# Flamingo block with sparse experts: the last three expert tiles behind a branch, and each tile's rows added to the output by two DMAs of half rows

## The chip, the cores and the metric

The kernel runs on one core of one Trainium2 chip. The metric is the device time of one execution in microseconds (us). Engines are named as in the profile: PE does matmuls (PEld loads its weights), DVE, ACT and POOL are the vector, scalar and GpSimd engines, and SP only issues DMAs here. Each engine takes its instructions in the order in which they stand in its queue; engines and DMAs wait for each other through semaphores.

## The reference

Two gated blocks run over x of 4 x 512 tokens by 512 numbers, each a mixing step and a feed-forward step, all added to x. The first three steps (a gated int8 product, a ternary feed-forward and an attention of 16 heads) don't change here. The last step is the one the change touches: a mixture of experts, in which each of the 2048 tokens takes its two best of eight experts.

```python
logits = router_in @ router_w.T
probs = jax.nn.softmax(logits, axis=-1)
topw, topi = jax.lax.top_k(probs, TOP_K)                    # TOP_K = 2, E = 8
topw = topw / jnp.sum(topw, axis=-1, keepdims=True)
cw = jnp.zeros((T, E), flat.dtype).at[jnp.arange(T)[:, None], topi].add(topw)
g = jnp.einsum('td,edf->tef', flat, gate_w)                 # D = 512, F_E = 256
u = jnp.einsum('td,edf->tef', flat, up_w)
a = jax.nn.silu(g) * u
expert_out = jnp.einsum('tef,efd->ted', a, down_w)
y = jnp.einsum('ted,te->td', expert_out, cw) * SCALE
...
x = x + jnp.tanh(g_ffn[1]) * y
```

## The kernel before, in words

The first 1340 us or so are the first three steps and the attention, with PE full nearly throughout. What follows concerns the experts' stage, which begins while the attention's last heads still run and lasts to the end.

**Tiles.** The 4096 pairs of a token and an expert are sorted by expert into tiles of P = 128 rows. How many rows an expert has is known only at run time, so there are NSEG = 39 tiles, the most that could be needed; every tile's work is written out in the program, and the tile's expert number is read into a register (L1086) to pick the weights. Tiles 0 to 15 (part "a") are full tiles of rows from the first twelve token tiles, so that they can start before the last batch is through the attention. Tiles 16 to 38 (part "b") take the rest. `sort` runs once for each part, in steps (`yield`) beside other work, and leaves in `found[j]` the row numbers `ids` (128 on partitions, one column for each tile), the expert `owner_i` and a mask `owned` of the experts. Rows of a tile that belong to nobody get a number out of bounds.

**One tile's way.** `fetch`/`gather` (L1072, an indirect DMA that POOL issues) brings 128 rows of 512 numbers and 8 weights from the table `xtab` into `xg`, of which there are eight buffers. `weigh_rows` (L1081, L1082, on DVE) picks each row's weight of its expert. The rows are turned, either by PE (`by_tensor`, L1184 and a copy on ACT) or by DVE transposes and 16 SP DMAs (L576, L1175) for four tiles together. `hide` does the eight gate/up matmuls (L1089), the silu on ACT (L1090) and the product with the row's weight on DVE (L1091). `turn_hidden` turns the hidden rows on PE (L1184, copy on DVE L1185). `expert_out` does the four down matmuls (L1211), copies the sum to `y` on ACT (L1215; three buffers), and POOL issues an indirect DMA that adds the 128 rows of 512 numbers, 2 KB each, into `out` (L1216). Row numbers out of bounds are skipped.

**Order.** The loop at L1245 writes the order out by hand: in step j it fetches tiles ahead of their use (4 or 10 tiles), does the gate/up matmuls of tile j, turns the rows of tile j + 1 if PE does that, turns the hidden rows of tile j - 1 and puts out tile j - 2. In the last steps the order is bent so that the last tile's gate/up matmuls stand behind tile 36's and 37's down matmuls. On POOL's queue an add is followed by the gathers of that step.

**Adds in a chain.** Two tiles can hold the same token, so an add must not run while another is under way. The list `written` holds the last add, and the next one waits until that has landed (`add_manual_dep`). The first add of each part also waits for the stores of x to `out` that it adds to.

**The framework.** Semaphores are set by a tile framework, which also tracks reads and writes of tensors itself and puts waits between instructions that touch the same data.

Of the kernel before, what the change touches and what calls it, by code (L numbers as in the profile page):

```python
# [9 lines left out]
F32 = mybir.dt.float32  # L10
BF16 = mybir.dt.bfloat16
AF = mybir.ActivationFunctionType
ALU = mybir.AluOpType
AX = mybir.AxisListType

P = 128
B, S, D = 4, 512, 512
NT = S // P
# [23 lines left out]
NE, TOPK, FE = 8, 2, 256  # L42
# [3 lines left out]
TOK = B * S  # L46
TT = TOK // P
NSEG = (TOK * TOPK + NE * (P - 1)) // P
NA, TA = 16, 12
NB = NSEG - NA  # L50
ROW = D + NE
F32R = mybir.dt.float32r
I32 = mybir.dt.int32
# [3 lines left out]
def kernel(  # L57
# [21 lines left out]
    nc = tc.nc  # L79

    cp = ctx.enter_context(tc.tile_pool(name="const", bufs=1))
# [17 lines left out]
    def place_in(w, at, n):  # L99

        flat = w.rearrange("p e k f -> p (e k f)")
        return flat[:, at : at + n]
# [37 lines left out]
    def acc_tile():  # L140
        sums_in[0] += 1
        return bank(4 + sums_in[0] % 4)

    def small(n, tag):
        return sm.tile([P, n], F32, tag=tag, name=tag)
# [63 lines left out]
    with tc.tile_pool(name="q8", bufs=1) as q8, tc.tile_pool(name="l0", bufs=2) as l0, tc.tile_pool(  # L209
        name="w0", bufs=1  # L210
# [420 lines left out]
    def load_queries(n):  # L631
        th = la.tile([P, ROW], F32, tag="wq", name="wq")
        th = th[:, : KD * HD].rearrange("p (k n) -> p k n", k=KD)
        nc.gpsimd.dma_start(th, wq[:, n * HD : (n + 1) * HD].rearrange("(k p) n -> p k n", p=P))  # L634
        return th
# [80 lines left out]

    xtab = dram.tile([TOK + P, ROW], F32, name="xtab")
    yacc = out.rearrange("b s d -> (b s) d")
    rwT = cp.tile([P, KD, NE], F32, name="rwT")
    before = cp.tile([P, NE, NE], F32, name="before")  # L720
    ones_b = cp.tile([P, P], BF16, name="ones_b")
# [10 lines left out]
    def router_constants():  # L732
# [24 lines left out]

        zero = place_in(gu, 4 * SLOT + 512, ROW)
        nc.gpsimd.memset(zero, 0.0)
# [5 lines left out]
    stores = []  # L765
# [93 lines left out]
    def exclusive(v, tag):  # L859

        lower = sm.tile([P, NE, NE], F32, tag="ahead", name="lower")
        nc.vector.tensor_tensor(lower, before, v.unsqueeze(1).to_broadcast([P, NE, NE]), ALU.mult)
        t = small(NE, tag)
        nc.vector.tensor_reduce(t, lower, AX.X, ALU.add)
        return t

    def tiles_of(nt, shift):

        ps = work_tile()
        nc.tensor.matmul(ps[:, :NE], lhsT=ones_b, rhs=past[:, nt, :], start=True, stop=True)  # L870
        t = small(NE, "tiles")
        nc.vector.tensor_scalar(t, ps[:, :NE], 1.0 / P, shift, ALU.mult, ALU.add)
        nc.vector.tensor_scalar(t, t, ROUND, None, ALU.add)
        nc.vector.tensor_scalar(t, t, -ROUND, None, ALU.add)
        return t
# [3 lines left out]
    def full_tiles():  # L879
# [10 lines left out]
        nc.vector.tensor_scalar(base, first, float(P), None, ALU.mult)  # L890
        return last, base, limit, (ALU.is_ge, FAR)

    def other_tiles():
        tiles = tiles_of(TT, (P - 1) / (2 * P))
        nc.vector.tensor_tensor(tiles, tiles, taken, ALU.subtract)
        first = exclusive(tiles, "first")
        nc.vector.tensor_scalar(first, first, float(NA), None, ALU.add)
        last = small(NE, "last")
        nc.vector.tensor_tensor(last, first, tiles, ALU.add)
        limit = small(NE, "limit")  # L900
        nc.vector.tensor_scalar(limit, taken, float(P), None, ALU.mult)
        base = small(NE, "base")
        nc.vector.scalar_tensor_tensor(base, first, float(P), limit, ALU.mult, ALU.subtract)
        return last, base, limit, (ALU.is_lt, -FAR)

    found = {}

    def sort(pool, part, nt, c0, n, spans):
# [30 lines left out]
        nc.vector.tensor_reduce(owner, done, AX.X, ALU.add)  # L939
        owner_i = cp.tile([P, n], I32, name=part + "owner_i")  # L940
        nc.vector.tensor_scalar(owner_i, owner, NE - 1.0, None, ALU.min)
        owned = cp.tile([P, n, NE], F32, name=part + "owned")
        nc.vector.tensor_tensor(
            owned,
            owner.unsqueeze(2).to_broadcast([P, n, NE]),
# [5 lines left out]
        for s in range(TOPK):  # L951
            mine = pool.tile([P, nt, NE], F32, tag=part + "mine", name="mine", bufs=1)
# [19 lines left out]
        for s in range(TOPK):  # L972
            mine = slice(s * nt, (s + 1) * nt)
# [31 lines left out]
        nc.vector.scalar_tensor_tensor(none, ps[:, :n], -1.0, none, ALU.add, ALU.add)  # L1005
        ids = cp.tile([P, n], I32, name=part + "ids")
        nc.vector.tensor_tensor(ids, none, ps[:, n : 2 * n], ALU.add)
        for j in range(n):
            found[c0 + j] = (ids[:, j : j + 1], owner_i[0:1, j : j + 1], owned[:, j, :])
        yield  # L1010


# [2 lines left out]
    def step_beside():  # L1015
        if beside:
            try:
                next(beside[0])
            except StopIteration:
                beside.pop(0)  # L1020
# [45 lines left out]

    def gather(j, xg):

        ids, _, owned = found[j]
        table = xtab[: TA * P, :] if j < NA else xtab[:, :]  # L1070
        tc.keep_in_program_order(
            nc.gpsimd.indirect_dma_start(xg, None, table, bass.IndirectOffsetOnAxis(ap=ids, axis=0))  # L1072
        )
        return xg, owned
# [21 lines left out]
    hidden, first = {}, {}  # L1096
# [17 lines left out]
    for i in range(LAST + 3):  # L1114
        b, n = divmod(i, NHEAD)
# [13 lines left out]
        if i == LAST:  # L1129
            while beside:  # L1130
                step_beside()
            for j in range(len(first_hid)):
                first_rows[j] = gather(j, la.tile([P, ROW], F32, tag="wq", name="xg"))
        if i > LAST:
# [13 lines left out]

    by_tensor = {j for j in range(NSEG) if j < 2 * NT or j // NT == NA // NT or j >= NSEG - NSEG % NT}
    blocks_of, turned_in, got = {}, {}, {}

    def fetch(j):
        got[j] = gather(j, mo.tile([P, ROW], F32, tag="xg", name="xg", bufs=8))

# [31 lines left out]
    def prepare(j):  # L1188
        if j in by_tensor and j not in hidden and j not in turned_in:
            dst = mo.tile([P, KD * P], F32, tag="xgT", name="xgT", bufs=2)  # L1190
            turned_in[j] = turn_by_tensor(got[j][0], KD, dst, nc.scalar.copy)
            weigh_rows(j, *got.pop(j))

    def hide(j):
        if j not in hidden:
            prepare(j)
            h = mo.tile([P, FE], F32, tag="hid", name="hid", bufs=3)
            hidden[j] = expert_in(j, turned_in.pop(j), h)

    def turn_hidden(j):  # L1200
        e, h = hidden.pop(j)
        hT = turn_by_tensor(h, NF, mo.tile([P, NF * P], F32, tag="hidT", name="hidT", bufs=3))
        waiting[j] = (e, hT)

    written = []

    def expert_out(j):
        e, hT = waiting.pop(j)
        ps = acc_tile()
        for f in range(NF):  # L1210
            nc.tensor.matmul(  # L1211
                ps, lhsT=hT[f], rhs=dn[:, bass.ds(e, 1), f, :], start=(f == 0), stop=(f == NF - 1)
            )
        y = mo.tile([P, D], F32, tag="y", name="y", bufs=3)
        nc.scalar.copy(y, ps)  # L1215
        add = nc.gpsimd.indirect_dma_start(  # L1216
            yacc,
            bass.IndirectOffsetOnAxis(ap=found[j][0], axis=0),
            y,
            None,  # L1220
            bounds_check=TOK - 1,
            oob_is_err=False,
            compute_op=ALU.add,
        )
        if j in (0, NA):
            written.extend(stores[-1:] if j else stores[: B - 1])
        for w in written:
            tc.add_manual_dep(
                add.ins,
                w.ins.name,  # L1230
                mybir.DependencyInfo(mybir.DependencyClass.Sync, mybir.DependencyReason.DATA),
                reason="adds to what is there",
            )
        written[:] = [add]

    beside += [route(B - 1, mo), sort(mo, "b", TT, NA, NB, other_tiles)]
    hidden.update(first)
    waiting = {}

    lead = {j: 4 if j in by_tensor else 10 for j in range(len(first), NSEG)}  # L1240
    TURN = 7
    to_fetch = sorted(lead, key=lambda j: (max(j - lead[j], 0), j))
    to_turn = [j for j in to_fetch if j not in by_tensor]

    for j in range(NSEG + 1):  # L1245
        known = NSEG if len(found) == NSEG else NA
        for t in [t for t in to_fetch if t - lead[t] <= j and t < known]:
            fetch(t)
            to_fetch.remove(t)
        while to_turn and to_turn[0] - TURN <= j and to_turn[0] in got:  # L1250
            turn_rows(to_turn.pop(0))


        if j < NSEG - 1:
            for i in range(NT) if j == 0 else (j,):
                hide(i)
        if j and j + 1 < NSEG:
            prepare(j + 1)
        if j:
            turn_hidden(j - 1)  # L1260
        for i in (j - 2,) if j < NSEG - 1 else (j - 2, j - 1) if j == NSEG - 1 else (j - 1,):
            if i >= 0:
                expert_out(i)
        if j == NSEG - 1:
            hide(j)
        step_beside()
        step_beside()
        if j == NA - 4:
            while beside:
                step_beside()  # L1270


# [33 lines left out]
```

## Time and profile before

| | |
|---|---|
| median of 3 runs | 1577.73 us (1575.53 to 1578.02) |
| the profiled execution | 1579.8 us, with a span of 1578.0 us |
| PE busy | 1493.4 us, 95% |
| DVE, ACT, POOL busy | 908.2, 559.0, 422.1 us |
| granted TensorE clock, mean | 0.989 |
| add of a tile, POOL's part (L1216) | 39 times, 1.55 to 1.63 us |
| first and last add start at | 1357.85 and 1570.03 us |
| gather of a tile, POOL's part (L1072) | 39 times, 0.94 to 1.05 us |
| copy of a tile's sum to y (L1215) | 0.586 us |

The span is the time from the profiled execution's first instruction to its last; the execution itself took 1.8 us more. "Busy" is the time in which an engine runs instructions; of an indirect DMA only the part in which POOL writes its descriptors counts as busy, and the flight of the data afterwards is seen only in who waits for it. In lists of waits, "A <- B: 115.6, 35, 11.0" says that A stood idle until B came, 115.6 us in total, 35 times, 11.0 us at the longest. In a timeline each line has its start, its duration, the instruction, and in brackets the idle time ahead of it and what ended that.

### The profile page before, as it was taken

To read this page: it belongs to the slowest core of one execution; us is meant where nothing else is said; L and a number is where in the kernel's file an instruction comes from. 1 tells how busy PE (TensorE), PEld (TensorE's weight loads), DVE (VectorE), ACT (ScalarE), POOL (GpSimd) and SP (SyncE) were. 2 spreads that over 40 slices of the span, in tenths; PEclk is the share of its full clock that TensorE was granted. 3 is DMA by queue.
4 is the path that set the end of the run, shared out by engine and by line. 5 is a ranking of instruction groups with operands and counts; after the bars stand their busy time and mean duration, and the time that the engine had idled before them with its cause. 6 is when DMAs were issued, how large, how long until landed. Compare 5 with 4: busy or idle time off the path is not lost. (4 is left out here: it accounts for less than half of the span.)

```text
span 1578.0 us, 16041 instructions
## 1 busy us (share of the span) xinstructions
PE 1493.4 (95%) x4339; PEld 750.1 (48%) x4348; DVE 908.2 (58%) x2350; ACT 559.0 (35%) x1150; POOL 422.1 (27%) x546
## 2 busy tenths in 40 slices
PE   4888898899999999999999999999999998999997
PEld 2444656666544444444444444444444443455563
DVE  5898737556175555575655675655777552643311
ACT  3554453434243333353333353333433331412111
POOL 2232314352311122141131141131231112345332
PEclk9999999999999999999999999999999999999999
DMA  8633111013355445485455575574675653656642
GB/s 296 217 118 129 47 40 61 28 41 101 126 161 140 140 137 161 134 221 151 123 158 138 148 203 140 132 188 132 191 199 134 162 129 88 166 112 141 127 75 34
DMA packets 111512, 211.90 MB, mean 134 GB/s; under 512 B 29296, under 2 KB 33392, under 8 KB 111424
## 3 DMA queue, kind: packets, MB, share of 16 engines
q0 software_dynamic: 33408, 98.54, 23.9%
q1 hardware_dynamic: 70224, 100.74, 22.9%
q10 hardware_dynamic: 7792, 11.60, 2.2%
q8 instruction: 37, 0.61, 0.2%
q14 instruction: 51, 0.42, 0.1%
HBM read 96.14 MB, written 35.72 MB: 84 GB/s over the span
## 5 line engine op out<-in xcount | busy, mean ns | idle before, releaser
L673 DVE CUSTOM_DVE_ANT_0 e<-bank,mask_b 128x512 f32<-128x512 f32 x256 | 175.0, 688 | 245.3 <-PE bank L668 245.2
L668 PE MATMUL bank<-kT,qT 128*128 128x512 f32 x512 | 231.1, 593 | 0.0
L707 PE MATMUL bank<-wo,oT 128*128 128x512 f32 x512 | 230.7, 592 | 0.3 <-ACT oT L697 0.3
L693 PE MATMUL bank<-eT,v 128*128 128x512 f32 x512 | 230.4, 592 | 0.5 <-DVE nmax L673 0.5
L676 ACT ACTIVATE e<-e,nmax 128x512 f32<-128x512 f32 x256 | 184.3, 720 | 81.6 <-DVE nmax L673 74.7
L655 PE MATMUL bank<-gu,wq 128*128 128x512 f32 x384 | 174.9, 594 | 1.2 <-DVE nmax L673 1.2
L570 DVE STREAM_TRANSPOSE blocks<-e 128x512 f32<-128x512 f32 x256 | 158.9, 677 | 27.4 <-DMA eT<-blocks 22.6
L693 PEld LDWEIGHTS bank<-eT,v 128*128 128x128 f32 x512 | 97.3, 190 | 123.8 <-issue 110.3
L668 PEld LDWEIGHTS bank<-kT,qT 128*128 128x128 f32 x512 | 97.0, 190 | 123.1 <-issue 115.0
L707 PEld LDWEIGHTS bank<-wo,oT 128*128 128x128 f32 x512 | 97.1, 190 | 122.7 <-issue 120.3
L697 ACT COPY oT<-bank 128x512 f32<-128x512 f32 x64 | 37.5, 585 | 315.2 <-PE bank L693 297.1
L655 PEld LDWEIGHTS bank<-gu,wq 128*128 128x128 f32 x384 | 72.3, 190 | 91.9 <-issue 81.8
L634 POOL DMA_DIRECT2D wq<-in_L_xattn_Wq_dram x64 | 48.8, 763 | 246.1 <-PE bank L655 223.6
L684 DVE TENSOR_SCALAR e<-e,rt 128x512 f32<-128x512 f32 x256 | 107.9, 484 | 2.1
L649 POOL DMA_DIRECT2D wo<-in_L_xattn_Wo_dram x64 | 36.4, 570 | 269.6 <-PE bank L707 263.1
L659 ACT ACTIVATE qT<-bank 128x512 f32<-128x512 f32 x64 | 38.2, 597 | 171.6 <-PE bank L655 165.9
L448 PE MATMUL bank<-pjT,hT 128*128 128x512 f32 x320 | 86.4, 405 | 5.4 <-DVE hT L473 5.4
L461 PE MATMUL bank<-xfT,fcT 128*128 128x512 f32 x320 | 89.7, 410 | 0.0
L1089 PE MATMUL bank<-gu,turned 128*128 x192 | 87.3, 597 | 0.0
L500 PE MATMUL bank<-dn,gu 128*128 128x512 f32 x128 | 67.6, 644 | 10.9 <-ACT dn L502 5.0
L1211 PE MATMUL bank<-dn,hidT 128*128 x156 | 74.5, 601 | 1.6 <-DVE hidT L1185 1.6
L472 POOL TENSOR_TENSOR r<-r 128x512 f32<-128x512 f32 x40 | 41.8, 1047 | 107.7 <-ACT hT L471 83.3
(360 smaller groups left out, 1925.0 us busy)
## 6 DMA issues: line engine op xcount, KB each, us to landing
eT<-blocks SPq DMA_DIRECT2D x1016, 64.0 KB
wq<-in_L_xattn_Wq_dram POOLq DMA_DIRECT2D x64, 256.0 KB
wo<-in_L_xattn_Wo_dram POOLq DMA_DIRECT2D x64, 256.0 KB
kd<-dn SPq DMA_DIRECT2D x32, 256.0 KB
vd<-dn SPq DMA_DIRECT2D x32, 256.0 KB
kT<-kd POOLq DMA_DIRECT2D x32, 256.0 KB
v<-vd POOLq DMA_DIRECT2D x32, 256.0 KB
turned<-blocks SPq DMA_DIRECT2D x96, 64.0 KB
```

What stands on the lines that cost most here:

```text
L448: nc.tensor.matmul(outs[t], lhsT=h[:, t * P : (t + 1) * P], rhs=pjT[:, j, :], start=(j == 0 and u == 0), stop=(j == NH - 1 and u == 1),)
L461: nc.tensor.matmul(ps, lhsT=fcT[:, i, j * P : (j + 1) * P], rhs=xT[u][:, i, :], start=(u == 0 and i == 0), stop=(u == 1 and i == KD - 1),)
L570: nc.vector.transpose(blocks[:, :, :, t, :].rearrange("p c s r -> p s c r"), src.rearrange("p (s c i) -> p s c i", c=NQ, i=Q))
L655: nc.tensor.matmul(ps, lhsT=th[:, i, :], rhs=xT[:, :, i, :], start=(i == 0), stop=(i == KD - 1))
L668: nc.tensor.matmul(ps, lhsT=qT[:, t * P : (t + 1) * P], rhs=kT, start=True, stop=True)
L673: nc.vector.tensor_tensor_reduce(e, ps, mask_b[b], -1.0, 3.0e38, ALU.add, ALU.min, nmax[:, t : t + 1])
L676: nc.scalar.activation(e, e, AF.Exp, bias=nmax[:, t : t + 1], scale=-1.0, accum_out=total[:, t : t + 1])
L684: nc.vector.tensor_scalar(es[:, t, :], es[:, t, :], rt[:, t : t + 1], None, ALU.mult)
L693: nc.tensor.matmul(ps, lhsT=v[:, s, :], rhs=eT[:, :, s, :], start=(s == 0), stop=(s == NT - 1))
L707: nc.tensor.matmul(sums[b][t], lhsT=oT[:, t * P : (t + 1) * P], rhs=to, start=(n == 0), stop=(n == NHEAD - 1))
L1089: nc.tensor.matmul(ps, lhsT=xgT[k], rhs=gu[:, bass.ds(e, 1), k, :], start=(k == 0), stop=(k == KD - 1))
L1211: nc.tensor.matmul(ps, lhsT=hT[f], rhs=dn[:, bass.ds(e, 1), f, :], start=(f == 0), stop=(f == NF - 1))
```

## The change

Four things change, all in the experts' stage.

The tiles are split at NSURE = 36 (4096 / 128 + 8 / 2). Tiles 0 to 35 run in the loop as before, whose last steps are now bent around tile 35. Tiles 36 to 38 stand behind a branch at the end: the number of tiles in use, `in_all`, is computed by the sort of part b, every engine loads it, and the three tiles run only if it is over 36. `by_tensor` names the same tiles among the first 36 as before.

The add of a tile is split into two DMAs of half rows. `out` is viewed as 4096 rows of 256 numbers (`halves`); half u of row r is row 2r + u of that view, and the sort computes these numbers as `half_ids`. The first DMA adds `y[:, 0:256]`, the second `y[:, 256:512]`. Each half has a list of its own, `written[u]`, so by hand each add is told to wait for the add of the same half of the tile before.

The mask `owned` is kept in BF16 and not in F32.

```diff
+NSURE = TOK * TOPK // P + NE // 2
...
+    halves = out.rearrange("b s (u d) -> (b s u) d", u=2)
...
+        nc.vector.tensor_copy(in_all, last[:, NE - 1 :])
...
-        owned = cp.tile([P, n, NE], F32, name=part + "owned")
+        owned = cp.tile([P, n, NE], BF16, name=part + "owned")
...
+        half_ids = cp.tile([P, 2, n], I32, name=part + "half_ids")
+        for u in range(2):
+            nc.vector.tensor_scalar(half_ids[:, u, :], ids, 2.0, float(u), ALU.mult, ALU.add)
...
-        add = nc.gpsimd.indirect_dma_start(
-            yacc,
-            bass.IndirectOffsetOnAxis(ap=found[j][0], axis=0),
-            y,
-            None,
-            bounds_check=TOK - 1,
-            oob_is_err=False,
-            compute_op=ALU.add,
-        )
-        if j in (0, NA):
-            written.extend(stores[-1:] if j else stores[: B - 1])
-        for w in written:
-            tc.add_manual_dep(
-                add.ins,
-                w.ins.name,
-                mybir.DependencyInfo(mybir.DependencyClass.Sync, mybir.DependencyReason.DATA),
-                reason="adds to what is there",
+
+        for u in range(2):
+            mine = slice(u * D // 2, (u + 1) * D // 2)
+            add = nc.gpsimd.indirect_dma_start(
+                halves,
+                bass.IndirectOffsetOnAxis(ap=found[j][3][u], axis=0),
+                y[:, mine],
+                None,
+                bounds_check=2 * TOK - 1,
+                oob_is_err=False,
+                compute_op=ALU.add,
             )
-        written[:] = [add]
+            if j in (0, NA):
+                written[u].extend(stores[-1:] if j else stores[: B - 1])
+            for w in written[u]:
+                tc.add_manual_dep(
+                    add.ins,
+                    w.ins.name,
+                    mybir.DependencyInfo(mybir.DependencyClass.Sync, mybir.DependencyReason.DATA),
+                    reason="adds to what is there",
+                )
+            written[u][:] = [add]
...
-    for j in range(NSEG + 1):
+    for j in range(NSURE + 1):
...
+    n = nc.values_load(in_all[0:1, :], min_val=1, max_val=NSEG)
+    with tc.If(n > NSURE):
+        for j in range(NSURE, NSEG):
+            fetch(j)
+        for j in range(NSURE, NSEG):
+            hide(j)
+            turn_hidden(j)
+            expert_out(j)
```

The loop's other uses of NSEG become NSURE in the same way.

More of the change, by code (lines that the diff above doesn't have):

```diff
@@ L891, in full_tiles @@
         return last, base, limit, (ALU.is_ge, FAR)
+    in_all = cp.tile([P, 1], I32, name="in_all")
     def other_tiles():
@@ L1007, in sort @@
         nc.vector.tensor_tensor(ids, none, ps[:, n : 2 * n], ALU.add)
+        half_ids = cp.tile([P, 2, n], I32, name=part + "half_ids")
+        for u in range(2):
+            nc.vector.tensor_scalar(half_ids[:, u, :], ids, 2.0, float(u), ALU.mult, ALU.add)
         for j in range(n):
-            found[c0 + j] = (ids[:, j : j + 1], owner_i[0:1, j : j + 1], owned[:, j, :])
+            where = [half_ids[:, u, j : j + 1] for u in range(2)]
+            found[c0 + j] = (ids[:, j : j + 1], owner_i[0:1, j : j + 1], owned[:, j, :], where)
         yield
@@ L1067, in gather @@
     def gather(j, xg):
-        ids, _, owned = found[j]
+        ids, _, owned, _ = found[j]
         table = xtab[: TA * P, :] if j < NA else xtab[:, :]
@@ L1146 @@
     mo = ctx.enter_context(tc.tile_pool(name="moe", bufs=1, reuse_waits="tile"))
-    by_tensor = {j for j in range(NSEG) if j < 2 * NT or j // NT == NA // NT or j >= NSEG - NSEG % NT}
+    by_tensor = {j for j in range(NSEG) if j < 2 * NT or j // NT == NA // NT or j >= NSURE - NSURE % NT}
     blocks_of, turned_in, got = {}, {}, {}
@@ L1203, in turn_hidden @@
         waiting[j] = (e, hT)
-    written = []
+    written = [[], []]
     def expert_out(j):
@@ L1238 @@
     waiting = {}
-    lead = {j: 4 if j in by_tensor else 10 for j in range(len(first), NSEG)}
+    lead = {j: 4 if j in by_tensor else 10 for j in range(len(first), NSURE)}
     TURN = 7
@@ L1251 @@
             turn_rows(to_turn.pop(0))
-        if j < NSEG - 1:
+        if j < NSURE - 1:
             for i in range(NT) if j == 0 else (j,):
                 hide(i)
-        if j and j + 1 < NSEG:
+        if j and j + 1 < NSURE:
             prepare(j + 1)
@@ L1260 @@
             turn_hidden(j - 1)
-        for i in (j - 2,) if j < NSEG - 1 else (j - 2, j - 1) if j == NSEG - 1 else (j - 1,):
+        for i in (j - 2,) if j < NSURE - 1 else (j - 2, j - 1) if j == NSURE - 1 else (j - 1,):
             if i >= 0:
                 expert_out(i)
-        if j == NSEG - 1:
+        if j == NSURE - 1:
             hide(j)
```

## The prediction

> **What bounds the kernel now.** I read the page first, then the windows of the expert stage (from 1357.85, where the first tile's add starts), then the waits, POOL's timeline and last the chain that ended last. Differences under 0.2% (3.2 us) are about what a measurement of this kernel can't tell from no change. The windows of the expert stage:
>
> ```profile
> core 0: us, PE busy (x) PEld busy (x) DVE busy (x) ACT busy (x) POOL busy (x), PEclk, DMA share, GB/s
> ...
> 1400.00:1450.00 50.00, 50.00 (x143) 28.45 (x143) 15.12 (x46) 11.08 (x22) 27.16 (x22) 1.00 0.67 142
> 1450.00:1500.00 50.00, 46.88 (x117) 26.86 (x116) 16.70 (x43) 7.76 (x16) 21.04 (x16) 0.97 0.58 116
> 1500.00:1540.00 40.00, 40.00 (x107) 24.24 (x106) 6.94 (x19) 7.17 (x15) 14.09 (x11) 1.00 0.44 78
> 1540.00:1560.00 20.00, 20.00 (x63) 10.81 (x62) 3.83 (x11) 5.26 (x10) 5.77 (x4) 1.00 0.37 58
> 1560.00:1578.00 18.00, 7.49 (x18) 2.78 (x16) 0.90 (x2) 2.14 (x4) 5.11 (x4) 0.82 0.02 1
> ```
>
> PE is full to 1560, but for 3.1 us lost in 1450 to 1500. So a tile costs PE's time: eight gate/up matmuls (3.60), two turns of the hidden rows (0.38), four down matmuls (1.88), less their overlaps, which PE's timeline puts at 5.4 to 5.8 us a tile. In the last row the DMAs move almost nothing (share 0.02, 1 GB/s): the adds of the last three tiles write no rows. The reference's inputs say the same: the router's counts are 487, 437, 466, 667, 425, 511, 460, 643 rows, which fill 4+4+4+6+4+4+4+6 = 36 tiles, and the 36th (tile 35) has 3 rows. So 36 > NSURE = 36 is false, and the branch isn't taken.
>
> The adds are not the bound, but they are close to it. From the waits from 1335 on:
>
> ```profile
> POOL out_dram L1216 <- ACT y L1215: 115.6, 35, 11.0
> POOL out_dram L1216 <- DMA out_dram<-y,bids: 10.7, 3, 4.6
> ```
>
> 35 of the adds wait for their y, one for another ACT step and three for the add before them to land. The three are the price list for a chained add. From POOL's timeline:
>
> ```profile
> 1472.97 1.59 POOL L1216 DMA_INDIRECT out_dram<-y,bids  x1 [3.23 <-ACT y L1215]
> ...
> 1479.71 1.59 POOL L1216 DMA_INDIRECT out_dram<-y,bids  x1 [3.86 <-DMA out_dram<-y,bids]
> ...
> 1484.87 1.59 POOL L1216 DMA_INDIRECT out_dram<-y,bids  x1 [2.28 <-DMA out_dram<-y,bids]
> ```
>
> Start to start, an add that waits for its forerunner takes 6.74 and 5.16 us here, and 6.14 at 1503.94 to 1510.08. One add of a full tile is thus nearly as long as PE's 5.4 to 5.8 us for a tile. An add is mostly flight: POOL is busy 1.57 us with it (the line's median), but in the trace's records of landings its semaphore is full 4.4 to 5.1 us after the start, about 4.7 in the middle. The chain that ended last shows the smallest one:
>
> ```profile
> 1566.23 0.19 issue
> 1566.42 2.71 DMA out_dram<-y,bids
> 1569.13 0.03 issue
> 1569.15 0.02 POOLq L1216
> 1569.17 0.63 issue
> 1569.80 1.78 POOLq L1301
> ```
>
> Add 37 has no rows and lands after 2.71 us. Until POOL starts the next, at 1570.03, another 0.90 pass, and between the two adds before it, at 1562.95 and 1566.42, 3.47 - 2.71 = 0.76.
>
> **The change part by part.** *The last three tiles.* Nothing runs in them any more. PE's timeline has the gate/up groups of tiles 36 and 37 and their turns ahead of tile 35's down matmuls, and 38's behind. y of tile 35 would be there at about 1553 and not at 1558.6 (two gate/up groups of 3.5 and about 1.3 of turns go; about 2.4 of tile 35's own silu, product, turn and copy, 0.38 + 0.47 + 0.38 + 0.42 plus hand-overs, come uncovered). Alone, with one add landing after 3.3 (the landing records have 3.28 for tile 35's 3 rows) and the 5.3 that today lie between the last landing (1570.03 + 2.71 = 1572.74) and the end (1578.0), the span would be 1553.2 + 3.3 + 5.3 = 1562: a gain of some 16 us, if the adds kept up.
>
> *The branch.* Five loads of n (PE's value load of an expert number, L1086, has a median of 304 ns) and a compare, on engines that have nothing behind it but the end. SP's load stands ahead of its last transfers and waits only for in_all, long ready. No conditional jump is in the trace; by its nearest row I take 0.5 us in the tail, 0 to 5.
>
> *half_ids, in_all, owned in BF16.* A few DVE instructions (0.15 to 0.2 each by L1081 and L1082) beside a DVE that is idle two thirds of 1400 to 1500: nothing.
>
> *The halves.* This decides. The text of the change gives each half its own list, written[0] and written[1]. But the instructions as built say something else: every second half waits on the semaphore of its own tile's first half, and every first half on that of the previous tile's second half (and on ACT's y). Both halves write the tensor out at rows that are known only at run time, and the dependency tracker of the framework orders them by itself, on top of the lists. So 36 x 2 = 72 half adds stand in ONE chain, and the wait is on POOL's in-order queue; what is queued behind it there are the gathers, and through y's three buffers ACT's copy, and then PE's banks.
>
> A link's price: the flight L of a half (128 rows of 1 KB), which no row shows. Below it is the empty add, 2.71; above it the full one, 4.7. The number of rows is that of the full add, only their length halves. In the records of packets a full add's rows take 178 ns each, eight in a row on each DMA engine (1.4 us of 4.7); halving these entirely gives 4.0, not at all 4.7. I take 4.2, nearer to the full row. To it come 0.76 from a landing to the next tile's first half (the row above; two waits), and for the second half, whose wait is a single one as most waits for y are, 0.3 (adds start about 0.27 behind their y's end), up to 0.76. A tile: 2 x 4.2 + 0.76 + 0.3 = 9.46 us against PE's 5.4 to 5.8. So the chain is the bound from the first tile on: 35 x 9.46 = 331.1; tile 35 itself, 2 x 3.28 + 0.3 = 6.9; about 3 off for other tiles that are partly filled. Last landing: 1357.85 + 331.1 + 6.9 - 3 = 1692.8. Behind it 5.3 + 0.5: span 1698.6. The profiled execution was 1579.8 for a span of 1578.0, and the median of the runs, 1577.73, is 0.3 below that span, so I put the time at **1698 us**.
>
> The gathers don't add to it. One that stands behind both halves of a tile starts L + 0.3 + 1.9 = 6.4 after the tile's first half; it lands about 4.9 later (4.0 to 5.8 in the landing records), and in today's trace some 4 us of product, gate, turn and down matmul lie between that and the y of two tiles on: 15.3, while the chain takes 18.9 for two tiles. The 16 us of the last three tiles vanish too: PE ends early and waits.
>
> The Trainium skill, DMA: Bandwidth & Descriptors, section Anatomy of one DMA, gives a DMA issued by GpSimd 2.0 us plus bytes over 436 GB/s: 2.3 for a half of 131 KB and 2.6 for a whole add. An estimate from it would be 2 x 2.3 + 1.06 = 5.7 a tile, just PE's pace, and a time near 1570. This trace has 2.71 for an add of no bytes and 4.7 for a whole one, so I don't use it. [...]
>
> **The rivals.** *One chain, but halves fly almost like empty adds.* For it: 2.71 of 4.7 is there without a row. Against it: tile 35's 3 rows already cost 3.28, and the count of rows stays 128. At L = 3.3 a tile is 7.7: 1357.85 + 35 x 7.7 + 6.9 + 5.8 = 1640. At 2.71, 6.5 a tile, 1595: the floor of the chain case, still slower.
>
> *One chain, and halves fly like whole adds in traffic.* L = 4.7 and 0.76 twice: 10.9 a tile, 1752. The starts of 6.14 and 6.74 apart speak for it; that the gathers are spread over a longer time, so that traffic is thinner, speaks against it.
>
> *Two chains after all: the other side.* If a second half starts as soon as POOL has issued the first, a pair costs 1.57 + 0.30 more on POOL and flies in parallel. Its place: the gather behind it starts 1.87 later, and in 1450 to 1500, where PE already loses 3.1 us to waits that begin with a gather's landing, each of the 4.7 loops of two tiles (10.7 us) loses up to 1.87: 0 to 8.8, I take 7. The tail gains: 1562 + 1.9 (second half) + 0.5 = 1564.4. Together 1571, range 1564 to 1573: faster by 0.3% to 0.9%. It decides once a pair of halves with its restart is under PE's 5.4 to 5.8, so that the chain never binds. Against it stand the waits as built, one by one.
>
> *The change doesn't do what it says* in that the branch is taken: not with 36 tiles. If it were, 3 x 2 empty halves of 3.5 each and a cold gather would put 25 us more on the end.
>
> **How the numbers follow.** One chain at L from 3.6 to 4.6: 0.86. One chain with faster or slower halves, 1595 to 1655 and 1740 to 1752: 0.08. Two chains: 0.05, 0.04 of it faster. An equal time needs one chain at a pair's cost of some 6 us, below the floor, 0.01, or two chains with all their costs, the 0.01 that is left of them. The range: L = 3.6 with 0.3 gives 8.3 a tile and 1657; L = 4.6 with 0.5 gives 10.5 and 1735 to 1740. It leaves out the far rivals, about 0.14 together with what I have not thought of. Faster by over 0.2%: 0.04, within: 0.02, slower: 0.94.
>
> **What would show it.** In the changed profile POOL's adds have 72 entries, wait in the waits table mostly for "DMA out_dram<-y", some 60 to 70 times and for over 200 us in total, and stand alternately about 4.5 and 5.0 us apart. PE is no longer full: about 0.6 busy from 1370 on, ending its last matmul some 10 to 15 us before the end. DMA share in the stage falls from 0.4 to 0.67 to two thirds of that. The chain that ended last is made of DMA out_dram pieces with 0.3 to 0.8 of issue between them, over 15% of the span, where today it has 0.3%. Wrong would be: second halves that start 1.9 us after the first (two chains), pairs at under 6 us, or a PE that still sets the pace; or a flight outside 3.6 to 4.6.

## The result and the profile after

The changed kernel takes 1676.13 us (1673.48 to 1677.34, 5 runs) against 1577.73 us (1575.53 to 1578.89, 5 runs). The ratio is 1.0617, with a 95% interval from 1.06 to 1.0634: slower by 98 us. The profiled execution has a span of 1671.8 us and took 1673.55 us, one of the two shortest of the five. (The experiments were run in three groups, e1 to e4, e5 to e8 and e9 to e11, on two chips; each is compared with the kernel before in its own group, where that took 1583.76, 1580.88 and 1578.90 us. The ratios are those of the record; the quotient of two medians differs from them by up to 0.1%.)

The windows of the changed kernel's expert stage, with the same columns as before:

```profile
1400.00:1450.00 50.00, 35.38 (x105) 20.79 (x101) 7.65 (x25) 5.64 (x12) 22.68 (x16) 0.86 0.41 71
...
1600.00:1640.00 40.00, 15.96 (x30) 7.08 (x28) 2.23 (x5) 2.92 (x6) 14.40 (x10) 0.70 0.27 31
1640.00:1672.00 32.00, 0.00 (x0) 0.00 (x0) 0.00 (x0) 0.58 (x1) 9.29 (x6) 0.52 0.14 17
```

PE was full in 1400 to 1450 and now is busy 35.38 of 50; in the last 32 us it has nothing to do at all, while POOL still issues adds. POOL's timeline shows what it issues, two tiles of the middle:

```profile
1514.52 1.58 POOL L1228 DMA_INDIRECT out_dram<-y,bhalf_ids  x1 [1.51 <-DMA out_dram<-y,bhalf_ids]
1518.56 1.55 POOL L1228 DMA_INDIRECT out_dram<-y,bhalf_ids  x1 [2.46 <-DMA out_dram<-y,bhalf_ids]
1520.41 1.02 POOL L1081 DMA_INDIRECT xg<-xtab,bids  x1 [0.30 <-issue]
1522.93 1.58 POOL L1228 DMA_INDIRECT out_dram<-y,bhalf_ids  x1 [1.50 <-ACT hid L1099]
1526.92 1.55 POOL L1228 DMA_INDIRECT out_dram<-y,bhalf_ids  x1 [2.42 <-DMA out_dram<-y,bhalf_ids]
```

The second half of a tile starts 4.0 us after the first, not 1.9 us, and it was a DMA that ended POOL's wait: the landing of the first half. The next tile's first half starts 4.4 us later again. (At 1522.93 the profile names an ACT step as the releaser; the start fits the landing of the half before, as at the others.) A pair takes 8.4 us here and 8.63 us on average (1355.75 to 1657.71 in 35 tiles), against PE's 5.4 to 5.8. The waits from 1335 on say the same:

```profile
POOL out_dram L1228 <- DMA out_dram<-y,bhalf_ids: 66.0, 28, 3.3
ACT y L1224 <- DMA out_dram<-y,bhalf_ids: 57.8, 8, 8.0
POOL out_dram L1228 <- DMA out_dram<-y,ahalf_ids: 46.8, 20, 3.2
POOL out_dram L1228 <- ACT y L1224: 39.7, 11, 10.8
```

Before, three adds waited for a landing by this table, 10.7 us in all; now 48 do, 112.8 us. The table understates both, because it puts a wait for several semaphores down to one of them. By the trace's records of landings, 69 of the 71 later adds now start 0.27 to 0.83 us behind the landing of the add before. In the kernel before, 21 of 38 adds already did so (0.74 to 0.83 us behind it, with their y there for 0.3 us or more), so the chain of adds set the start of about half of them. The second line is the same jam one station up the road: ACT can't copy the next sum, because y's three buffers are held by adds that haven't landed.

### The profile page after: what moved, and what is told of

It is laid out like the page before. It is cut to its first block, busy times and chain, and to the rows that moved or that the text cites. A ratio compares the mean times of both kernels' runs of the same rounds, so it can differ in the third digit from the quotient of the medians.

```text
span 1671.8 us, 16010 instructions
## 1 busy us (share of the span) xinstructions
PE 1497.4 (90%) x4294; PEld 746.9 (45%) x4294; DVE 906.8 (54%) x2343; ACT 553.7 (33%) x1141; POOL 470.2 (28%) x576
## 5 line engine op out<-in xcount | busy, mean ns | idle before, releaser
L1228 POOL DMA_INDIRECT out_dram<-y,bhalf_ids x40 | 62.2, 1556 | 95.6 <-DMA out_dram<-y,bhalf_ids 66.0
L1220 PE MATMUL bank<-dn,hidT 128*128 x144 | 83.7, 713 | 1.6 <-DVE hidT L1194 1.6
```

Of the source, the lines that this page charges most:

```text
L1228: add = nc.gpsimd.indirect_dma_start(halves, bass.IndirectOffsetOnAxis(ap=found[j][3][u], axis=0), y[:, mine], None, bounds_check=2 * TOK - 1,
```

## The experiments

**Theory:** the whole loss is one chain of 72 flights, and it is one chain because the framework orders every add into out behind the last one, whatever lists the kernel keeps. **Rivals:** the halves themselves are slow (two flights hinder each other, or rows of half length cost something), or part of the loss sits in the branch and the new order of the last tiles, or POOL's second add of each tile delays the gathers.

**Two real chains (e1).** The framework is told that an add has no dependency on the last add of the other half; the lists by hand stay.

```diff
+            for other in added[1 - u]:
+                tc.declare_no_dep(add.ins, other.ins, reason="the other half of the rows")
             written[u][:] = [add]
+            added[u][:] = [add]
```

> The changed kernel, with one edit: the framework is told that a half's add needs no wait for the adds of the other half, so that each half waits only for the same half of the tile before (two real chains). Theory (the whole loss is the single chain of 72 flights that the framework's own tracking draws): the chain is no longer the bound, 36 flights of about 3.7 us with 0.75 between them fit under PE's 5.4 to 5.8 us a tile, second halves start 1.9 us after the first, and the time is about 1571 us (1564 to 1576), faster than before. Rival (two adds in flight hinder each other on the DMA engines or in POOL's queue, so that a pair still takes over 8 us): 1640 to 1680 us. Rival (POOL's 1.9 us more in each tile delay the gathers so much that they become the bound): 1585 to 1620 us.

Measured: 1575.26 us against 1583.76, ratio 0.995 (0.9936 to 0.9964). One declaration turns 6% slower into 0.5% faster. POOL's timeline of that kernel:

```profile
1537.53 1.55 POOL L1229 DMA_INDIRECT out_dram<-y,bhalf_ids  x1 [1.97 <-ACT y L1225]
1539.38 1.55 POOL L1229 DMA_INDIRECT out_dram<-y,bhalf_ids  x1 [0.30 <-issue]
1542.90 1.55 POOL L1229 DMA_INDIRECT out_dram<-y,bhalf_ids  x1 [1.97 <-ACT y L1225]
...
1557.54 1.55 POOL L1229 DMA_INDIRECT out_dram<-y,bhalf_ids  x1 [1.23 <-DMA out_dram<-y,bhalf_ids]
1559.39 1.55 POOL L1229 DMA_INDIRECT out_dram<-y,bhalf_ids  x1 [0.30 <-issue]
1562.02 1.55 POOL L1229 DMA_INDIRECT out_dram<-y,bhalf_ids  x1 [1.08 <-DMA out_dram<-y,bhalf_ids]
```

Second halves now start 1.85 us after the first, waiting for nothing but POOL; the pairs stand 5.37 us apart, PE's pace, and wait for y. Only the last three pairs, and two in the middle, wait for a landing. A half in company lands after 3.79 us at the median, 3.73 in the changed kernel: two flights at once don't hinder each other. Half rows and the branch are both still there, so they can't make the loss either. Delayed gathers are the one rival of which something may be left, and it is small: PE loses 6.9 us in the first 100 us from the first add, 4.9 of it in one wait, where the kernel before loses 3.5 up to 1557, and whole rows with the branch (e2 and e10, below) 6.0 and 4.2 in the first 180 us.

**Whole rows with the branch (e2, and again as e10).** The add is one DMA of whole rows as before; everything else is as in the changed kernel.

> The changed kernel with the add of a tile as one DMA of whole rows, as before; the branch for the last three tiles and all the rest stay. Theory: the branch part alone gains what the last three empty tiles cost, less its own tail; tile 35's y at about 1553 us, its add landed at about 1556.4, then the 8.2 us that the changed kernel's profile has between the last landing and the end: a span of about 1565, a time of 1564 to 1568 us. Rival (part of the loss sits in the branch: loads of the count, jumps, cold instructions): 1580 us or more. Rival (the last three tiles were hidden anyway): 1575 to 1579 us.

Measured: 1571.9 us, ratio 0.9932 (0.9917 to 0.9947). By the number that is over the theory's 1564 to 1568, but the kernel before took 6 us longer in this group, and 11 us below it is within the theory's 10 to 14. Its terms were off, and in opposite directions: tile 35's y was there at 1554.48 us, near the 1553 expected, but its add landed at 1564.87 and not at 1556.4, and behind that lay 5.0 us and not 8.2. Neither rival's time came. With whole rows, the branch and the new order of the last tiles gain 11 us, so they don't make the loss.

> The branch with whole rows once more, on the same chip as the form with the copy of a column of y: 0.68% (10 to 11 us) below the kernel before, as it was.

Measured: 1568.21 against 1578.9, ratio 0.993 (0.9918 to 0.9942), as the first time. Its gain is short of the 16 us that the prediction gave for the tiles if the adds keep up. They don't: the sums of the last tiles come sooner, and the whole adds fall behind. The timelines of ACT and POOL show it, here in e2:

```profile
1550.59 1.55 POOL L1226 DMA_INDIRECT out_dram<-y,bids  x1 [4.12 <-ACT hid L1099]
1553.90 0.58 ACT L1224 COPY y<-bank 128x512 f32<-128x512 f32 x1 [3.65 <-PE bank L1220]
1556.19 1.55 POOL L1226 DMA_INDIRECT out_dram<-y,bids  x1 [4.05 <-DMA out_dram<-y,bids]
1561.61 1.55 POOL L1226 DMA_INDIRECT out_dram<-y,bids  x1 [3.87 <-DMA out_dram<-y,bids]
```

and in the kernel before:

```profile
1558.05 0.59 ACT L1215 COPY y<-bank 128x512 f32<-128x512 f32 x1 [1.30 <-PE bank L1211]
1558.91 1.55 POOL L1216 DMA_INDIRECT out_dram<-y,bids  x1 [4.21 <-ACT y L1215]
```

These are tile 35's copy and its add: in e2 the add starts 7.1 us behind the end of the copy, in the kernel before 0.3 us. The link of a whole add, from its start to the next add's, is 5.4 to 5.7 us at the end of e2 (median flight 4.85), as long as PE's tile. So whole adds keep up with PE only just, before the change too, and the last ones queue up.

**The same without the branch (e3).** The loop ends at tile 35 and nothing stands behind it.

```diff
-    n = nc.values_load(in_all[0:1, :], min_val=1, max_val=NSEG)
-    with tc.If(n > NSURE):
-        ...
```

> As the run with whole rows and the branch, but without the branch and what stands behind it: 36 tiles and no more, which is enough for these inputs (a run that needed more tiles would lack them). It prices the branch by itself. Theory: in the changed kernel's profile POOL's step before the end (INC_SWDGE_SEM, 1.49 us) and its DRAIN come only after the last landing, while the kernel before starts its DRAIN beside the last add; without the branch the tail is 5.3 us again instead of 8.2: about 3 us less than with the branch, 1561 to 1564 us. Rival (the DRAIN takes as long as it must after the last landing, whatever stands ahead of it): the same time as with the branch, within 1 us.

Measured: 1571.91 us, ratio 0.9936 (0.9916 to 0.9956): the same as with the branch. Here the rival was right. In e2 POOL's last DRAIN takes 5.1 us after the branch, in e3 it takes 6.9 us without one; from the last add's start to the DRAIN's end there are 7.4 and 6.7 us. The branch costs less than these runs can tell.

**Halves in one chain, all 39 tiles (e4).** The changed kernel with NSURE = NSEG and without the branch.

> Halves in one chain as in the changed kernel, but all 39 tiles in the loop and no branch. Theory (the chain sets the time): three more tiles of two empty halves, 2 x 2.7 + 0.3 + 0.75 = 6.5 us each, so 19 us more than the changed kernel, less 3 us of the branch's tail: about 1692 us (1686 to 1698). Rival (the branch or the order of the last tiles takes part of the loss): below the changed kernel's 1676 us.

Measured: 1696.05 us, ratio 1.0712 (1.0693 to 1.0731). Against the kernel before that is 112 us more, where the changed kernel has 98: three empty tiles cost 14 us at the end of the chain (15 by the ratios), 16 were expected. In its timeline the empty halves start 3.0 and 3.5 us apart.

**Quarters in one chain (e5).** Four DMAs of 128 numbers for each tile: u runs over four, and the view and the row numbers are made with 4 and not 2.

> The changed kernel with four DMAs of quarter rows (512 bytes) for each tile, each with its own numbers and list, all in the one chain that the framework draws: 144 flights instead of 72. It sizes a flight by its row length. In the profiles a whole row's add lands after 4.9 us (median), a half's after 3.7, an empty one's after 2.7. Theory (a fixed 2.7 us, and the rest in proportion to the bytes): a quarter lands after 3.2 to 3.3, a tile takes 4 x 3.25 + 0.75 + 3 x 0.27 = 14.6 us, the 36 tiles end at about 1357 + 36 x 14.6 + 8 = 1890 us. Rival (the number of rows sets a floor, about 3.6 us, whatever their length): 16.0 us a tile, 1940 us.

Measured in one run: 1906.82 us, near the theory's 1890 and not the rival's 1940. One tile in POOL's timeline:

```profile
1606.72 1.57 POOL L1228 DMA_INDIRECT out_dram<-y,bhalf_ids  x1 [1.39 <-ACT y L1224]
1610.36 1.55 POOL L1228 DMA_INDIRECT out_dram<-y,bhalf_ids  x1 [2.07 <-DMA out_dram<-y,bhalf_ids]
1614.03 1.55 POOL L1228 DMA_INDIRECT out_dram<-y,bhalf_ids  x1 [2.12 <-DMA out_dram<-y,bhalf_ids]
1617.58 1.55 POOL L1228 DMA_INDIRECT out_dram<-y,bhalf_ids  x1 [2.00 <-DMA out_dram<-y,bhalf_ids]
```

Four links of about 3.6 us, with a median flight of 3.28 by the records of landings. So the flights of 128 rows of 0, 512, 1024 and 2048 bytes are 2.71, 3.28, 3.73 and 4.66 to 4.87 us: 2.7 us that no shortening of the rows takes away, and some 1.05 us for each KB of a row. The number of rows counts too: tile 35's three rows alone land after 3.26 to 3.28 us as whole rows and after 2.85 to 2.88 as halves. Each link more on a chain pays the 2.7 again.

**A copy ahead of the add (e6).** POOL copies one column of y first, so that the wait for ACT stands on the copy, and the add has a single wait.

```diff
         nc.scalar.copy(y, ps)
+        nc.gpsimd.tensor_copy(small(1, "ready"), y[:, D - 1 :])
```

> The changed kernel with one tiny POOL copy of a column of y ahead of a tile's adds, so that the wait for ACT's y stands on that copy, and the first half's add has only one wait, that for the second half of the tile before. It tests the two restarts, 0.75 us with two waits and 0.27 with one. Theory (POOL serves two waits by an instruction of its own and only then prepares the add): 35 times 0.5 us goes, less some tenths for the copies: 12 to 18 us less than the changed kernel, that is 82 to 88 us above the kernel before. Rival (the 0.75 is the time POOL needs between two adds in any case, and the copy comes on top): 98 us or more above the kernel before.

Measured: 1668.6 us, ratio 1.0543 (1.0517 to 1.057), 88 us above the kernel before where the changed kernel has 98. The median from a second half to the next first half falls from 4.51 to 4.06 us, and from the first to the second, 4.00 before, it is 4.07: with one wait all links are alike. It holds, at the weak end of the range.

**The copy with whole rows (e7, and again as e11) and with two chains (e8).**

> The branch with whole rows, and the tiny POOL copy of a column of y ahead of each add. In the profile of the branch with whole rows the last three adds stand 5.4 to 5.6 us apart behind a y that is there already, so 0.5 us less in each link brings the end forward. Theory: 2 to 5 us below the branch with whole rows, which was 11.9 us below the kernel before: 13 to 17 us below it. Rival (only the last links wait, and POOL's copies cost as much as they save): within 1.5 us of the branch with whole rows.

> Two real chains of halves, and the tiny POOL copy of a column of y ahead of each tile's adds. Theory (two real chains cost nothing but POOL's second add of 1.9 us a tile, and gain where the whole adds queue up at the end): 9 to 14 us below the kernel before, no better than whole rows with the same copy, since PE sets the pace and the last second half lands 1.9 us later. Rival (halves with two chains are the better form once restarts are short): 3 us or more below whole rows with the same copy.

Measured: e7 has 1570.82 us, ratio 0.9929 (0.9909 to 0.9949), e8 has 1575.81, ratio 0.9965 (0.9951 to 0.9979). For e7 the rival holds by the time; for e8 neither the theory's 9 to 14 us nor the rival, as it is only 5 us below. Two chains with the copy are no better than two chains without.

> The branch with whole rows and the tiny POOL copy of a column of y ahead of each add, beside the branch with whole rows on the same chip. Theory (each link of the chain of adds is 0.25 us shorter, 5.43 for 5.68 us from start to start in the profiles, and the last add starts 199.6 us behind the first and not 203.1): 2 to 4 us below the branch with whole rows. Rival (its gain is lost in the gathers that stand behind the copy's wait): within 1.5 us of it.

Measured: 1566.71 us, ratio 0.9918 (0.9905 to 0.9931), 1.5 us below e10 on the same chip, with intervals that overlap. Whether the copy gains anything with whole rows stays open: the two pairs of runs put it at 1.5 us and, by the ratios of e7 and e2, at 0.5 us.

**First halves only (e9).** The second halves' adds are left out; 36 links.

> The changed kernel without the adds of the second halves (the second 256 numbers of each row of out get nothing from the experts): one chain as in the changed kernel, but of 36 links and not 72. Theory (the number of chained flights makes the loss): a link of 3.75 + 0.75 = 4.5 us is under PE's 5.4 to 5.8, so PE sets the pace again; with shorter links in the tail than whole rows have (4.5 for 5.6, three of them), the time is 12 to 18 us below the kernel before, as much as or a little more than the branch with whole rows (11 below). Rival (rows of half length, their numbers or the view of out cost something in themselves): not below the kernel before by more than 5 us.

Measured: 1560.84 us against 1578.9, ratio 0.9885 (0.9871 to 0.9899), 18 us below, at the end of the theory's range. A chain of 36 adds of half rows, which also moves half the bytes, is not slower than one of whole rows but faster, so rows of half length, their numbers and the view are not what costs. It is also about what the last three tiles are worth when the adds keep up: until tile 32 they start 1.2 to 3.0 us behind the landing of the add before, but for one, and wait for y. Only the last three queue, tile 35's by 2.7 us behind its y. They are the last links in POOL's timeline:

```profile
1539.96 1.55 POOL L1228 DMA_INDIRECT out_dram<-y,bhalf_ids  x1 [2.88 <-DMA out_dram<-y,bhalf_ids]
1544.42 1.55 POOL L1228 DMA_INDIRECT out_dram<-y,bhalf_ids  x1 [2.92 <-DMA out_dram<-y,bhalf_ids]
1549.07 1.55 POOL L1228 DMA_INDIRECT out_dram<-y,bhalf_ids  x1 [3.09 <-DMA out_dram<-y,bhalf_ids]
```

They are 4.5 us apart where whole rows need 5.5. Between this and the two chains lie 10 us by the ratios, and 12.8 in the two profiles from the first add to the end. Of these, 5.8 are in PE's waits early in the stage (6.9 us lost against 1.1), 1.9 in the last second half and 2.7 behind the last landing (8.05 us against 5.36); where the other 2.4 lie stays open.

The best complete kernel of the study is whole rows with the branch, 0.7% to 0.8% below the kernel before, with or without the copy.

## Why the prediction was right

**One chain.** This was the step that decided, and it came from the waits of the built instructions, not from the text of the change. By the text the two lists are two chains; e1 shows what the text would have given, 0.995, and the changed kernel what the built waits give. Rows of half length (e9) take no part in the loss, and the branch (e2, e3) none but the 2 us of its tail, below. The reading of the kernel before was too mild, though: "35 of the adds wait for their y" is the waits table's count, and by the landings 21 of 38 adds hung on the add before. It didn't matter to the sum, which puts every tile on the chain anyway.

**The sum.** Predicted 1698 us, measured 1676: inside the range, the loss of 98 us overrated by 22. By its terms, in the profile of 1671.8 us: the first add started at 1355.75 and not 1357.85 (2.1 less); 35 tiles took 302.0 and not 331.1 - 3 = 328.1 (26.1 less); tile 35 took 6.0 and not 6.9 (0.9 less); and behind the last landing, at about 1663.7, lie 8.05 and not 5.8 us (2.25 more). Together that is some 26.8 less than the 1698.6 predicted, which is the span. The median run is some us longer than the profiled one.

**The mis-sized term** is the flight of a half, "I take 4.2, nearer to the full row". It is 3.73 at the median, and 3.77 on average over the 35 tiles, which alone makes 2 x 0.43 x 35 = 30 us. The lower end, 4.0, was wrong as well, and the time fell inside the range only because that was drawn from 3.6: it took only the packets' own 1.4 us as what can shrink. The packets of 1 KB do take 102 ns where those of 2 KB take 178, which gives eight times 76 ns, 0.6 us; the flight shrank by 0.9 to 1.1. Where the other 0.3 to 0.5 us comes from the records don't show. The two rows that the prediction had, 2.71 for no bytes and 4.7 for 2 KB, lie on the line that the quarters confirm; the middle of them, 3.7, would have been the better choice. The two restarts, from a landing to the next add's start, were right: 0.27 us for one wait and 0.76 for two at the median, and e6 moved one into the other.

**The tail.** "5.3 + 0.5" carried over a DRAIN that before ran beside the last add. In the changed kernel it starts behind the last landing, after a step of POOL of 1.49 us (INC_SWDGE_SEM) that belongs to the branch:

```profile
L1285 POOLq INC_SWDGE_SEM  x1: 1492/1492/1492, 1664.0 to 1664.0; - x1
...
L1322 POOLq DRAIN  x3: 46/103/5417, 1665.5 to 1671.5; - x3
```

In e4, with the same chain but without the branch, 5.8 us lie behind the last landing, so the branch costs 2.2 of the changed kernel's 98 us. In e2, where that step began before the last add had landed, 5.0 us lie behind it, and the branch cost nothing that these runs can tell.

**The signs to look for.** The 72 adds, their alternating links and PE's idle end came as told; PE is busy for 0.66 of the time from 1370 on, where about 0.6 was told. Four readings were off. The links are 4.0 and 4.5 us and not 4.5 and 5.0, which is the mis-sized flight again. The waits table has 48 waits for a landing, 112.8 us, and not 60 to 70 and over 200. The count was right by the landings, which give 69; the time was not, since POOL is busy issuing for 1.55 us of each flight, and with a gather for 1.3 more, and only the rest is a wait. The chain that ended last covers some 11% of the span and not 15%. And PE ends its last matmul at 1638.2, 34 us before the end and not 10 to 15: three buffers of y let it run three tiles ahead, and the adds of tiles 33 to 35 take from 1641.05 to 1663.7.

**The other rivals.** Two chains were put at 1571, 7 us below the kernel before; e1 measured 8.5 below. So the number was near, but by two errors that cancel: the delayed gathers were put at 7 us and cost 3.4 at most (6.9 lost against 3.5), and the gain at the tail was put at 13.6 and is smaller, since the last pairs queue 4.5 to 4.6 us apart. The estimate from the Trainium skill, DMA: Bandwidth & Descriptors, section Anatomy of one DMA, would have put the single chain near 1570: its 2.0 us and 436 GB/s are 0.7 us under the empty flight here, and far from the 1.05 us for 128 KB, which is 125 GB/s. The measurement decides. The same page's Rules for kernel authors say of many small transfers to coalesce them into one large one. That holds in e2 and e10: one add of whole rows beats two halves in one chain by 7%. Against two chains the 0.2% between e1 and e2 are at the edge of what these runs can tell.

## What to carry to other kernels

Count the links of a chain before the bytes: an indirect add here costs 2.7 us of flight and 0.3 to 0.8 us of restart however few bytes it moves, so halving one on a serial chain makes its share of the chain half as long again (8.5 us for 5.5). Splitting pays only if the parts truly run side by side, and that stands in the waits of the built instructions; a list of dependencies by hand adds edges and takes none away. A stage's second bound is found by dividing: 5.5 us for a link against 5.4 for a tile says that the next gain on PE's side will queue up there. A table that puts each wait down to one cause can hide such a bound; when each landed, set beside the start of what waits for it, shows it.

## What the runs showed of the hardware

A PE that waits was here also a slower PE: in 1400 to 1450 the granted clock was 1.00 before and 0.86 after, and 0.70 in 1600 to 1640. The eight down matmuls at 1608.67, behind 6.3 us of idle time, took 6.15 us, with a granted clock of 0.52 in 1610 to 1614; the kernel before has 3.60 for eight at 1558.07, at a clock of 1.00. It cost nothing here, since PE was ahead of the adds: from tile 27 on a tile's y is there 16 to 17 us before its first add starts. The first line is of the kernel before, the second of the changed one.

```profile
1558.07 3.60 PE L1211 MATMUL bank<-dn,hidT 128*128 x8
1608.67 6.15 PE L1220 MATMUL bank<-dn,hidT 128*128 x8
```

A wait for two semaphores cost POOL about half a microsecond more than a wait for one ahead of an indirect DMA (0.76 and 0.27 us from the landing to the start). With two, one wait is a step of its own (EVENT_SEMAPHORE), which ends at 1656.98 us ahead of the changed kernel's add at 1657.71; with one, the DMA itself waits. What POOL does in the half microsecond between the two steps the trace doesn't show.
